# A mixture-of-experts kernel whose head and tail are laid out anew: token blocks loaded and summed during the first unit, two load queues, and two of the last groups read back a unit later

## The chip, the cores and the metric

The kernel runs on one core of a Trainium2 chip. The metric is the device time of one execution in microseconds (us). Engines are named as in the profile: PE is the matrix engine TensorE, PEld its weight loads, DVE is VectorE, ACT is ScalarE, POOL is GpSimd, SP is SyncE, which here issues most of the DMA transfers.

## The reference

A gated feed-forward layer with eight experts and one shared expert is added to its input. All is fp32; x is 16 sequences of 256 tokens with 256 features, and the hidden width F is 1024.

```python
g = jnp.einsum('bsd,edf->ebsf', h, Wg)
u = jnp.einsum('bsd,edf->ebsf', h, Wu)
expert_outs = jnp.einsum('ebsf,efd->ebsd', jax.nn.silu(g) * u, Wd)
expert_output = jnp.einsum('be,ebsd->bsd', gating_probs, expert_outs)
shared = jnp.einsum('bsf,fd->bsd', jax.nn.silu(h @ Sg) * (h @ Su), Sd)
sg = shared_gate_prob[:, :, None]
return x + (1.0 - sg) * expert_output + sg * shared      # h is x
```

Every expert runs over every token; the gates are given as one number for each expert and sequence.

## The kernel before

**Units.** The work is cut into 72 units: 9 experts (the shared one last) x 2 halves of the hidden width (512 columns, four chunks of 128) x 4 groups `g0` to `g3` of four token blocks (one block is one sequence of 256 tokens). The group runs fastest, so a set of weights serves four units in a row. A unit has an up part (`unit_up`, L590), which makes the gated hidden values, and a down part (`unit_down`, L677), which multiplies them by the down weights; the down part of one unit lies between the up matmuls of the next.

**Up.** A contraction of 256 is two halves of 128. Four weight chunks against four token blocks would take 32 products of 128x256 for each of the gate and up matrices. The kernel evaluates chunks and blocks at the points -1, 0, 1, 2 and takes 26: eight on the diagonal (`diagonal`, L515, into the PSUM bank D) and three for each of six pairs (`offdiagonal`, L558). Of a pair, one product goes to a bank M; POOL subtracts two diagonal terms (`s<-pq,pq`), DVE adds the two into a bank X (`X<-M,s`), and two more products accumulate on X. ACT takes the silu (`sg<-X`), DVE multiplies (`h<-X,coef,sg`). This needs sums of weights (`load_base` L285 and `make_pair` L306, tags wb and wp, made anew for each expert half) and of tokens (`make_xd` L387, tag xd, after a transpose on PE; `make_xp` L470, tag xp: for each of six pairs two 128x256 operations of DVE, one of POOL, for some pairs a scaling on ACT). The token sums are made once for each group, in the first units; `keep` (L376) writes them to DRAM, and `load_xd` and `load_xp` read them back in every later unit.

**Unit 0** alone is done plainly, so that TensorE can begin before any sums exist: eight steps (`unit_up`, `n == 0`), each with one product of a gate chunk (bank X) and one of an up chunk (bank M) with two token blocks, four 128x512 matmuls by the profile for each. `make_raw` (L424) transposes and copies its four blocks, `load_raw` (L328) brings the raw second halves of the first weights. Until data comes, 16 matmuls on zeros run (L258).

**Down.** In a 2x2 block scheme seven products are made instead of eight (`ORDER`, L674), each into one of two PSUM banks dn. ACT copies a product to SBUF (`ev<-dn`, L729), and two DMAs of POOL for each unit (`total<-ev`, L743) accumulate four and three of them in DRAM, in one total for each group. In the last expert half (units 68 to 71) the totals are read back (`load_pieces` L759), into the buffers wb and wd (`IN_W`) for g0, g2 and into ev (`IN_EV`) for g1 and g3. For units 68, 69 and 70 the unit's own seven products are added to these pieces by DVE straight from the dn banks. `finish` (L786) makes seven combinations of the pieces (128x512 each, two on POOL and five on DVE), transposes the results back on PE (`dn<-...` L829), adds x on DVE (L838) and stores. For the last unit, the combinations, transposes and x are done ahead (`basis`), and `last_down` (L851) adds plain down products, in the banks dn and M by turns, and stores.

**What sets the order.** Nothing is ordered by hand. Every instruction is an operation of a `Plan` (L47) with an engine, an estimated length, a lag, a rank, buffers and dependencies. `Plan.run` simulates the engines, takes on each the ready operation of lowest rank whose buffers are free, and emits in that order; PE strictly follows rank. A unit is W = 12 ranks long. The resulting order on each engine and queue is fixed in the program. Ranks for the loads, sums and transposes are given in the main loop (L879 to L916), e.g.

```python
    make_raw(a, -14 + 3 * a)                                    # unit 0
    (make_xd if n < NG else load_xd)(g, a, r0 - W + 6 * a - 4)  # all others
```

so before the change the blocks of g1 and g2 are transposed two at a time (`a` is a pair of blocks), mostly in the unit before the one that uses them, and the six xp of g1 are made around the start of unit 1, of g2 around unit 2, of g3 around unit 3; those of g0, which unit 0 does not need, are made at its end for the use in unit 4.

Of the kernel before, what the change touches and what calls it, by code (L numbers as in the profile page):

```python
# [16 lines left out]
P = 128  # L17
# [17 lines left out]
class Op:  # L35
    def __init__(self, engine, length, lag, rank, emit, deps, new, uses):
        self.engine, self.length, self.lag, self.rank, self.emit = engine, length, lag, rank, emit
        self.new, self.uses = new, uses
        self.after = []
        self.missing = 0  # L40
# [6 lines left out]
class Plan:  # L47
# [9 lines left out]
    HOP = 0.25  # L57

# [7 lines left out]
    def add(self, engine, length, rank, emit, deps=(), new=(), uses=(), lag=None):  # L66
        lag = self.HOP if lag is None else lag
        op = Op(engine, length, lag, rank, emit, deps, list(new), list(uses))
        for b in [*op.new, *op.uses]:
            b.users += 1  # L70
        self.ops.append(op)
        return op

    def run(self):
# [19 lines left out]
        now = 0.0  # L94
        while left:
# [9 lines left out]
            for e in ready:  # L105
# [23 lines left out]
                idle[e] = end  # L129
                order.append(took)  # L130
# [17 lines left out]
def kernel(  # L148
# [56 lines left out]
    tags("xp", [P, 3, TB], 5)  # L205
# [52 lines left out]
    for n in range(16):  # L258
# [4 lines left out]
    def load(rank, dst, src, kb, deps=(), new=(), uses=(), lag=None):  # L263
        return add("SP", 0.6, rank, lambda: nc.sync.dma_start(dst(), src), deps, new, uses, lag=lag or 3 + kb / 150)
# [20 lines left out]
    def load_base(m, e, half, rank):  # L285
# [5 lines left out]
        lag = None if rank < 0 else 14  # L291
        u = load(rank, lambda: b[:, :, 0, :], src[0], 256, [], [b], lag=lag)
        v = load(rank, lambda: b[:, :, 1, :], src[1], 256, [], [], [b], lag=lag)
# [12 lines left out]
    def make_pair(m, e, half, k, rank):  # L306
# [15 lines left out]
        if d == 1:  # L322
            o = tt("POOL", rank, lambda: b[:, 1:3, :], rr, uu, ALU.subtract, 2 * P, [r, u], [], [b, w])
        else:
# [3 lines left out]
    def load_raw(rank):  # L328
# [4 lines left out]
                rank + 3 * m, lambda m=m: b[:, :, m, :],  # L333
                sources(0)[m][ts(1, P), 0 : 4 * P].rearrange("p (c q) -> p c q", q=P), 256,
                [], [b] if m == 0 else [], [b] if m else [],
# [5 lines left out]
    def load_down(e, half, rank):  # L341
# [3 lines left out]
            n: load(rank, lambda n=n: b[:, :, n, :], s[:, :, c, k, :], 128, [], [b] if n == 0 else [], [] if n == 0 else [b], lag=12)  # L345
# [30 lines left out]
    def keep(key, b, deps, rank, kb):  # L376
        d = dram.tile(list(b.shape), F32, tag=f"keep_{key}", name=f"keep_{key}")
        kept[key] = d
        keptop[key] = add(
            "SP", 0.6, rank, lambda: nc.sync.dma_start(d, b.buf.tile), deps, uses=[b.buf], lag=2.2 + kb / 200  # L380
        )

    class Shaped:
        def __init__(self, buf, shape):
            self.buf, self.shape = buf, shape

    def make_xd(g, a, rank):  # L387
        b = Buf("xd", f"xd_{g}_{a}")
        done = {}
        for n in range(2):  # L390
            i = 2 * a + n
            t = POINTS[i]
            xin = Buf("xio", f"xin_{g}_{i}")
            src = x[4 * g + i].rearrange("(h p) d -> p h d", p=P)
            ld = load(rank - 1, lambda xin=xin: xin[:, :, :], src, 256, [], [xin])
            pt = Buf("dn", f"xt_{g}_{i}")

            def transposes(pt=pt, xin=xin):
# [4 lines left out]
            tr = add("PE", 4 * TR, rank, transposes, [ld], [pt], [xin])  # L403
            y = add(
                "ACT", act(TB), rank, lambda n=n, pt=pt: nc.scalar.copy(b[:, 2 + n, :], pt[:, 1, :]), [tr],
                [b] if n == 0 else [], [pt] if n == 0 else [pt, b],
            )
            if t == 0:
                o = add(
                    "ACT", act(TB), rank, lambda n=n, pt=pt: nc.scalar.copy(b[:, n, :], pt[:, 0, :]), [tr, y],  # L410
                    [], [pt, b],
                )
            else:
                o = stt(
                    rank, lambda n=n: b[:, n, :], lambda n=n: b[:, 2 + n, :], -float(t),
# [4 lines left out]
        keep(f"d_{g}_{a}", Shaped(b, [P, 4, TB]), [o for v in done.values() for o in v], rank + 2, 512)  # L420
# [3 lines left out]
    def make_raw(a, rank):  # L424
# [3 lines left out]
        for n in range(2):  # L428
# [3 lines left out]
            ld = load(rank - 1, lambda xin=xin: xin[:, :, :], src, 256, [], [xin])  # L432
# [9 lines left out]
            def copy(n=n, pt=pt):  # L442
                (nc.vector.tensor_copy if n else nc.scalar.copy)(b[:, n : n + 3 : 2, :], pt[:, :, :])
# [3 lines left out]
                    ("ACT", "DVE")[n], act(2 * TB), rank, copy, [tr],  # L447
# [5 lines left out]
    def sum_raw(a, rank, after):  # L453
# [14 lines left out]
        keep(f"d_0_{a}", Shaped(b, [P, 4, TB]), [o for v in done.values() for o in v], rank + 1, 512)  # L468
# [495 lines left out]
```

## Time and profile before

The kernel took 2561.29 us (median of 3 runs, 2561.25 to 2561.4).

| profiled execution | us |
|---|---|
| its own time | 2560.55 |
| its span, first to last instruction | 2558.8 |
| PE busy | 2521.2 (99%) |
| DVE busy | 1894.3 (74%) |
| POOL busy | 1721.5 (67%) |
| ACT busy | 778.3 (30%) |
| a unit in the middle (start to start) | 34.46 |
| unit 0 / 1 / 2 / 3 | 53.72 / 46.60 / 41.43 / 37.37 |
| unit 69 / 70 / 71 with the drain | 40.46 / 40.35 / 58.25 |
| mean granted TensorE clock | 0.997 |

A profile row such as `X<-M,s 128x512` names the written tile, then those read, by their tags (a buffer's number is left out). `xN` is the number of instructions. Times are in us, the mean of a group in ns. "Idle before, releaser" is how long the engine had stood still and what ended it. In the table, a unit begins with its first matmul on the sums of pairs (`M<-xp,wp`), so the unit that comes first holds everything from the start of the span; matmuls are pipelined, and the pitch from start to start is what one takes of the engine's time.

### The profile page before, as it was taken

What the parts mean: (1) busy time and instruction counts of PE and PEld (TensorE: products, weight loads), DVE (VectorE), ACT (ScalarE), POOL (GpSimd) and SP (SyncE); (2) the same over time, 40 slices, a digit from 0 to 9 for tenths busy, and PEclk for the clock granted to TensorE, in tenths of its full rate; (3) what the DMA queues carried; (4) which work ended last, traced back from release to release, by engine and by line L of the source; (5) the groups of instructions that cost most, each with busy time, mean ns of one, the idle gap of its engine ahead of it and who ended that gap; (6) DMA issues with size and microseconds to landing.
All of it is one profiled execution on the core that took longest, in us unless ns stands there. A gap on an engine that the chain in (4) does not pass through costs nothing. (4 is left out here: it accounts for less than half of the span.)

```text
span 2558.8 us, 30286 instructions
## 1 busy us (share of the span) xinstructions
PE 2521.2 (99%) x9644; PEld 1822.6 (71%) x9644; DVE 1894.3 (74%) x3272; ACT 778.3 (30%) x1367; POOL 1721.5 (67%) x1638
## 2 busy tenths in 40 slices
PE   8899999999999999999999999999999999999998
PEld 4667777777777777777777777777777777777766
DVE  5886777777676877676777767677867776776787
ACT  2333333333233333323333332333333233333310
POOL 5686766767676767676766767576767676776653
PEclk9999999999999999999999999999999999999999
DMA  6455666666666666666666666656666666666652
GB/s 200 163 181 166 166 157 169 161 175 159 174 157 158 162 161 175 158 175 156 166 162 168 168 167 163 166 151 164 165 168 168 162 168 158 166 160 177 181 184 85
DMA packets 179089, 421.51 MB, mean 165 GB/s; under 512 B 15056, under 2 KB 84192, under 8 KB 170224
## 3 DMA queue, kind: packets, MB, share of 16 engines
q1 hardware_dynamic: 159280, 294.70, 34.9%
q0 software_dynamic: 19648, 124.86, 26.5%
q8 instruction: 76, 1.25, 0.2%
q14 instruction: 85, 0.70, 0.1%
HBM read 276.90 MB, written 142.61 MB: 164 GB/s over the span
## 5 line engine op out<-in xcount | busy, mean ns | idle before, releaser
L268 POOL TENSOR_TENSOR s<-pq,pq 128x512 f32<-128x512 f32 x852 | 1147.9, 1376 | 523.1 <-DVE X L268 502.9
L509 PE MATMUL dn<-h,wd 128*128 128x512 f32 x1988 | 1016.6, 593 | 0.0
L509 PE MATMUL X<-xp,wp 128*128 128x256 f32 x3408 | 878.2, 380 | 7.4 <-DVE X L268 7.4
L268 DVE TENSOR_TENSOR X<-M,s 128x512 f32<-128x512 f32 x852 | 590.6, 694 | 367.5 <-PE M L509 236.8
L509 PEld LDWEIGHTS X<-xp,wp 128*128 128x128 f32 x3408 | 647.8, 190 | 219.5 <-issue 108.1
L509 PE MATMUL D<-xd,wb 128*128 128x256 f32 x2272 | 584.6, 380 | 4.5 <-DVE h L273 3.4
L509 PEld LDWEIGHTS M<-xp,wp 128*128 128x128 f32 x1704 | 324.2, 190 | 345.7 <-issue 332.3
L273 DVE SCALAR_TENSOR_TENSOR h<-X,coef,sg 128x256 f32<-128x256 f32 x852 | 394.8, 478 | 214.3 <-PE X L509 163.8
L509 PE MATMUL M<-xp,wp 128*128 128x256 f32 x1704 | 507.7, 380 | 0.0
L729 ACT COPY ev<-dn 128x512 f32<-128x512 f32 x476 | 279.4, 587 | 666.8 <-PE dn L509 666.6
L509 PEld LDWEIGHTS D<-xd,wb 128*128 128x128 f32 x2272 | 431.6, 190 | 67.6 <-DVE h L273 4.3
L268 DVE TENSOR_TENSOR h<-h,h 128x512 f32<-128x512 f32 x426 | 468.6, 1126 | 0.0
L509 PEld LDWEIGHTS dn<-h,wd 128*128 128x128 f32 x1988 | 377.8, 190 | 51.5 <-POOL wb L268 0.2
L607 ACT ACTIVATE sg<-X 128x512 f32<-128x512 f32 x434 | 258.4, 595 | 149.9 <-PE X L509 124.9
L536 ACT COPY pq<-D 128x512 f32<-128x512 f32 x284 | 166.5, 586 | 440.8 <-PE D L509 432.2
L268 DVE TENSOR_TENSOR pq<-D,pq 128x256 f32<-128x256 f32 x568 | 224.0, 417 | 40.4 <-PE D L509 40.1
L743 POOL DMA_DIRECT2D total<-ev x128 | 113.1, 883 | 195.7 <-ACT ev L729 186.8
L268 POOL TENSOR_TENSOR h<-h,h 128x512 f32<-128x512 f32 x142 | 199.7, 1407 | 47.8 <-PE dn L509 31.0
L607 ACT ACTIVATE sg<-D 128x512 f32<-128x512 f32 x142 | 84.8, 597 | 472.9 <-DVE pq L268 472.9
L268 POOL TENSOR_TENSOR wp<-wb 128x128 f32<-128x128 f32 x216 | 140.4, 661 | 0.0
L273 DVE SCALAR_TENSOR_TENSOR h<-D,coef,sg 128x256 f32<-128x256 f32 x284 | 134.5, 474 | 0.0
L273 DVE SCALAR_TENSOR_TENSOR wp<-wb,wp 128x256 f32<-128x256 f32 x108 | 88.3, 819 | 0.0
(68 smaller groups left out, 501.7 us busy)
## 6 DMA issues: line engine op xcount, KB each, us to landing
xp<-keep_p SPq DMA_DIRECT2D x408, 384.0 KB, 4.0
total<-ev POOLq DMA_DIRECT2D x68, 1024.0 KB, 7.9
xd<-keep_d SPq DMA_DIRECT2D x136, 512.0 KB, 3.5
total<-ev POOLq DMA_DIRECT2D x68, 768.0 KB, 7.0
keep_p<-xp SPq DMA_DIRECT2D x24, 384.0 KB, 2.6
wb<-in_L_cond_Wg_dram SPq DMA_DIRECT2D x33, 256.0 KB, 4.5
wb<-in_L_cond_Wu_dram SPq DMA_DIRECT2D x33, 256.0 KB, 4.9
wd<-in_L_cond_Wd_dram SPq DMA_DIRECT2D x64, 128.0 KB, 3.7
```

Of the source, the lines that this page charges most:

```text
L268: return add(engine, length, rank, lambda: eng.tensor_tensor(o(), a(), b(), op), deps, new, uses)
L273: lambda: nc.vector.scalar_tensor_tensor(o(), a(), c() if callable(c) else c, b(), ALU.mult, op),
L509: lambda: nc.tensor.matmul(o(), w(), mv(), start=start, stop=stop, skip_group_check=onto),
L536: lambda: nc.scalar.copy(p_[:, 2 - 2 * a : 4 - 2 * a, :], bank[:, :, :]), ps,
L607: lambda: nc.scalar.activation(b[:, :, :], bank[:, :, :], AF.Silu), deps, [b], [bank],
L729: lambda ev=ev, at=at, bank=bank: nc.scalar.copy(ev[:, at, :], bank.tile.rearrange("p a t -> p (a t)")),
L743: nc.gpsimd.dma_start(total[g][part], ev[:, 0:k, :], accum_op=ALU.add)
```

## The change

Parts, in the order of time:

1. **Start of the program.** 9 instead of 16 matmuls on zeros. The first loads get a new order over two queues: SP brings x0, x1, the raw Wg, the first half of Wu, x2, x3, the second halves of Wg and Wu, then the eight blocks of g1 and g2 (into h buffers), the down weights and the blocks of g3; the queue of ACT brings the first half of Wg and the raw Wu. All four copies of raw tokens are on ACT (two were on DVE).
2. **Order on PE in unit 0.** x0 and x1 are transposed, then step 0 follows, then x2 and x3, then the other steps at a spacing of 2.6 ranks (it was 2). Between them the eight blocks of g1 and g2 are transposed one at a time (before, six blocks of unit 0 in pairs of two). From g3 on, a block has its own rank too (`rank + n / 2`).
3. **Token sums.** The six xp of g1 are made in unit 0 into xp buffers, those of g2 into ev buffers ("aside") and stored at once, to be read back for unit 2. g0's are made ahead of unit 4. Six xp buffers instead of five. For the first weights only, three pairs of each matrix are made with an ACT multiplication and a POOL subtraction in place of one DVE operation.
4. **End.** Units 68 and 69 (g0, g1) use the normal `unit_down` (copies on ACT, accumulating DMAs of POOL); the totals are read back a unit later, into wb and wd (`IN_W`). Unit 70 (g2) still adds to pieces, in ev. g3's pieces go to wb and wd. A third one of the seven combinations goes to POOL (`o` = 2), the output transposes have a rank and spacing of their own, and `last_down` uses the banks X and M.
5. **The planner.** Transfers carry their size (`kb`), and the simulation sends them one after the other; lags of loads change with it. This adds no instruction.

The numbers of matmuls and transposes are unchanged but for the zeros. Cut to its core (left out: the planner's bookkeeping, the lags of `load_down`, `keep` and stores, lines that only follow a renamed argument, and the class `Slice`, a 128x3x256 view of a part of an ev buffer):

```diff
@@ tags
-    tags("xp", [P, 3, TB], 5)
+    tags("xp", [P, 3, TB], 6)
...
@@ zero matmuls
-    for n in range(16):
+    for n in range(9):
...
@@ load
-    def load(rank, dst, src, kb, deps=(), new=(), uses=(), lag=None):
-        return add("SP", 0.6, rank, lambda: nc.sync.dma_start(dst(), src), deps, new, uses, lag=lag or 3 + kb / 150)
+    def load(rank, dst, src, kb, deps=(), new=(), uses=(), late=0, engine="SP"):
+        queue = {"SP": nc.sync, "ACT": nc.scalar}[engine]
+        return add(
+            engine, 0.5, rank, lambda: queue.dma_start(dst(), src), deps, new, uses, lag=2.2 + late, kb=kb
+        )
...
@@ load_base
-    def load_base(m, e, half, rank):
+    def load_base(m, e, half, rank, ranks=None):
...
-        lag = None if rank < 0 else 14
-        u = load(rank, lambda: b[:, :, 0, :], src[0], 256, [], [b], lag=lag)
-        v = load(rank, lambda: b[:, :, 1, :], src[1], 256, [], [], [b], lag=lag)
+        late = 0 if rank < 0 else 8
+        ru, rv = ranks or (rank, rank)
+        engine = "ACT" if ranks and m == 0 else "SP"
+        u = load(ru, lambda: b[:, :, 0, :], src[0], 256, [], [b], late=late, engine=engine)
+        v = load(rv, lambda: b[:, :, 1, :], src[1], 256, [], [], [b], late=late)
...
@@ make_pair
+        elif e == half == 0:
+            o = add(
+                "ACT", act(2 * P), rank, lambda: nc.scalar.mul(b[:, 1:3, :], uu(), float(d)), [r, u], uses=[b, w]
+            )
+            o = tt("POOL", rank, lambda: b[:, 1:3, :], rr, lambda: b[:, 1:3, :], ALU.subtract, 2 * P, [o], [], [b])
...
@@ load_raw
-    def load_raw(rank):
+    def load_raw(ranks):
...
-                rank + 3 * m, lambda m=m: b[:, :, m, :],
+                ranks[m], lambda m=m: b[:, :, m, :],
...
-                [], [b] if m == 0 else [], [b] if m else [],
+                [], [b] if m == 0 else [], [b] if m else [], engine=("SP", "ACT")[m],
...
@@ make_xd
-    def make_xd(g, a, rank):
+    def make_xd(g, a, rank, load_rank, sum_rank):
...
-            xin = Buf("xio", f"xin_{g}_{i}")
+            xin = Buf("h" if g < 3 else "xio", f"xin_{g}_{i}")
...
-            ld = load(rank - 1, lambda xin=xin: xin[:, :, :], src, 256, [], [xin])
+            ld = load(load_rank, lambda xin=xin: xin[:, :, :], src, 256, [], [xin])
...
-            tr = add("PE", 4 * TR, rank, transposes, [ld], [pt], [xin])
+            rank_n = rank + n / 2
+            tr = add("PE", 4 * TR, rank_n, transposes, [ld], [pt], [xin])
...
-                    rank, lambda n=n: b[:, n, :], lambda n=n: b[:, 2 + n, :], -float(t),
+                    sum_rank, lambda n=n: b[:, n, :], lambda n=n: b[:, 2 + n, :], -float(t),
...
@@ make_raw
-    def make_raw(a, rank):
+    def make_raw(a, rank, load_rank):
...
-            ld = load(rank - 1, lambda xin=xin: xin[:, :, :], src, 256, [], [xin])
+            ld = load(load_rank, lambda xin=xin: xin[:, :, :], src, 256, [], [xin])
...
-                (nc.vector.tensor_copy if n else nc.scalar.copy)(b[:, n : n + 3 : 2, :], pt[:, :, :])
+                nc.scalar.copy(b[:, n : n + 3 : 2, :], pt[:, :, :])
...
-                    ("ACT", "DVE")[n], act(2 * TB), rank, copy, [tr],
+                    "ACT", act(2 * TB), rank, copy, [tr],
...
@@ make_xp
-    def make_xp(g, k, rank):
+    def make_xp(g, k, rank, put_aside=False):
...
-        b = Buf("xp", f"xp_{g}_{k}")
+        if put_aside:
+            new = k % 2 == 0
+            buf = aside[g, k // 2] = Buf("ev", f"aside_{g}_{k}") if new else aside[g, k // 2]
+            b = Slice(buf, k % 2)
+        else:
+            new = True
+            buf = b = Buf("xp", f"xp_{g}_{k}")
...
-            [s, yj], uses=[b, tj],
+            [s, yj], uses=[buf, tj], more=0.3,
...
-        xp[g, k], xpop[g, k] = b, (s, n7, n6)
-        keep(f"p_{g}_{k}", Shaped(b, [P, 3, TB]), [s, n7, n6], rank + 2, 384)
+        if not put_aside:
+            xp[g, k], xpop[g, k] = b, (s, n7, n6)
+        keep(f"p_{g}_{k}", [P, 3, TB], b, buf, [s, n7, n6], rank + 2, 384)
...
@@ unit_up, n == 0
-                    r = 2 * step - 7 + m / 2
+                    r = 2.6 * step - 7 + m / 2
...
@@ finish
-    def finish(g, pieces, rank, store_it=True):
+    def finish(g, pieces, rank, out_rank, store_it=True):
...
-                "POOL" if o in (3, 4) else "DVE", rank, m[o][0], m[a][0], m[c][0], op, 2 * TB,
+                "POOL" if o in (2, 3, 4) else "DVE", rank, m[o][0], m[a][0], m[c][0], op, 2 * TB,
...
-                r = rank + 2 + (2 * row + bp) / 2
+                r = out_rank + 0.6 * (2 * row + bp)
...
@@ last_down
-            bank = Buf(("dn", "M")[step % 2], f"ld_{blk}_{h}")
+            bank = Buf(("X", "M")[step % 2], f"ld_{blk}_{h}")
...
@@ main loop
     for n, unit in enumerate(units):
         e, half, g = unit
         r0 = W * n
+        if n == 0:
+            make_raw(0, -14, -20)
+            load_base(0, e, half, -16, (-20, -16))
+            first_raw = load_raw((-19, -17.5))
+            load_base(1, e, half, -15, (-18, -15))
+            make_raw(1, -5.5, -17)
+        elif g == 0:
+            for m in range(2):
+                load_base(m, e, half, r0 - W + 3 * m - 8)
         if g == 0:
-            for m in range(2):
-                load_base(m, e, half, r0 - W + 3 * m - (8 if n else 4))
-                if n == 0 and m == 0:
-                    first_raw = load_raw(-12.5)
             for k in range(len(PAIRS)):
                 for m in range(2):
                     make_pair(m, e, half, k, r0 + 2 * k + m - (8 if n else -4))
             load_down(e, half, r0 + W - 8)
         if n == end:
             rows = load_rows(e, half, r0 - 2)
-        for a in range(2):
-            if n == 0:
-                make_raw(a, -14 + 3 * a)
-            else:
-                (make_xd if n < NG else load_xd)(g, a, r0 - W + 6 * a - 4)
+        if n == 1:
+            for a in range(2):
+                make_xd(g, a, -3.4 + 2 * a, -14, -3 + 2 * a)
+            for k in range(len(PAIRS)):
+                make_xp(g, k, 5 + k)
+            for a in range(2):
+                make_xd(2, a, 3.2 + 2 * a, -13, 5 + 2 * a)
+            for k in range(len(PAIRS)):
+                make_xp(2, k, 11 + k / 2, True)
+        elif n == 3:
+            for a in range(2):
+                make_xd(g, a, r0 - W + 6 * a - 4, r0 - W + 6 * a - 6, r0 - W + 6 * a - 7)
+            for k in range(len(PAIRS)):
+                make_xp(g, k, r0 + 2 * k - 5)
+        elif n == 4:
+            for a in range(2):
+                load_xd(g, a, r0 - W + 6 * a - 4)
+            for k in range(len(PAIRS)):
+                make_xp(g, k, r0 + 2 * k - 5)
+        elif n:
+            if n > 2:
+                for a in range(2):
+                    load_xd(g, a, r0 - W + 6 * a - 4)
+            for k in range(len(PAIRS)):
+                load_xp(g, k, r0 + 2 * k - 5)
         if n == end:
-            basis = finish(g, load_pieces(g, IN_EV, r0 - 2 * W + 3), r0 - 2 * W + 7, False)
-        if n:
-            for k in range(len(PAIRS)):
-                (make_xp if n < NG else load_xp)(g, k, r0 + 2 * k - 5)
+            basis = finish(g, load_pieces(g, IN_W, r0 - 2 * W + 1), r0 - 2 * W + 4, r0 - 2 * W + 10.3, False)
         hb, hops = unit_up(n, unit)
-        if n == 0:
-            for k in range(len(PAIRS)):
-                make_xp(g, k, 10 + k)
         if n == end:
             last_down(n, unit, hb, hops, rows, basis)
+        elif n == end - 1:
+            pieces = load_pieces(g, IN_EV, r0 + W - 1)
+            unit_down(n, unit, hb, hops, pieces)
+            finish(g, pieces, r0 + 2 * W + 1, r0 + 2 * W + 4.2)
         elif n > end - NG:
-            pieces = load_pieces(g, IN_EV if g == 1 else IN_W, r0 + W - 3)
-            unit_down(n, unit, hb, hops, pieces)
-            finish(g, pieces, r0 + 2 * W + 1)
+            unit_down(n, unit, hb, hops)
+            finish(g, load_pieces(g, IN_W, r0 + 2 * W + 2), r0 + 2 * W + (4, 11)[g], r0 + 2 * W + (11, 13.5)[g])
         else:
             unit_down(n, unit, hb, hops)
     last = {}
```

## The prediction

> **What bounds the kernel now.** I read the busy shares first, then the starts of the units, then the waits of TensorE in the few units that are longer than the rest. TensorE is busy all but 1% of the span:
>
> ```profile
> PE 2521.2 (99%) x9644; PEld 1822.6 (71%) x9644; DVE 1894.3 (74%) x3272; ACT 778.3 (30%) x1367; POOL 1721.5 (67%) x1638
> ```
>
> So no gain is to be had from the 65 units in the middle. A unit's start is its first M matmul in TensorE's timeline; cutting the span there gives this table of windows (length; busy of TensorE, its weight loads, DVE, ACT, POOL; clock; DMA share; GB/s). Rows 1 to 4 are units 1 to 4, row 5 is unit 68, the last three are units 69, 70 and 71 with the drain:
>
> ```profile
> 53.72:100.32 46.60, 38.20 (x146) 26.39 (x145) 41.10 (x74) 13.82 (x28) 30.79 (x31) 0.96 0.52 193
> 100.32:141.75 41.43, 37.24 (x141) 26.77 (x140) 33.01 (x57) 12.68 (x24) 23.80 (x22) 0.96 0.51 178
> 141.75:179.12 37.37, 34.92 (x133) 24.91 (x132) 34.46 (x54) 11.41 (x21) 32.13 (x37) 1.00 0.51 178
> 179.12:213.59 34.47, 34.47 (x134) 25.08 (x133) 25.10 (x45) 10.90 (x19) 21.94 (x20) 1.00 0.44 154
> 2385.28:2419.74 34.46, 34.46 (x133) 25.08 (x132) 23.18 (x43) 10.90 (x19) 19.41 (x16) 1.00 0.64 160
> 2419.74:2460.20 40.46, 37.88 (x149) 27.42 (x148) 35.66 (x59) 6.91 (x12) 21.39 (x17) 0.96 0.62 188
> 2460.20:2500.55 40.35, 36.81 (x150) 26.39 (x148) 34.88 (x58) 6.90 (x12) 22.70 (x16) 1.00 0.63 203
> 2500.55:2558.80 58.25, 48.91 (x201) 35.16 (x199) 43.20 (x66) 4.18 (x7) 21.79 (x16) 0.97 0.24 78
> ```
>
> A full unit takes 34.46. Useful work of the others, from TensorE's pitch (start to start: 1.72 for four 128x512, 0.86 for four 128x256, 0.434 for the four transposes of a token block): unit 0, 16 plain products x 1.72 + 8 D x 0.86 + 10 blocks x 0.434 = 38.7; units 1 and 2, 34.46 + 2 blocks = 35.3; units 69 and 70 36.2; unit 71 45.7 and a drain of 3.45 from its last matmul to the end. What is above that is lost: 15.0, 11.3, 6.1, 2.9 in units 0 to 3 and 4.2, 4.2, 9.1 in units 69 to 71. These 52.8 us are all that the change can reach; the floor is the start (below), near 2518.
>
> In unit 0, TensorE's timeline (start, length, idle before and its releaser) shows 13.2 us lost ahead of the first plain product (14.98 less four transposed blocks, 1.74):
>
> ```profile
> 13.25 1.94 PE L438 MATMUL dn<-ident,xio 128*128 128x128 f32 x8 [3.49 <-DMA xio<-in_x_dram]
> 14.98 2.49 PE L509 MATMUL X<-pq,wb 128*128 128x512 f32 x4
> ```
>
> In units 1 and 2 the waits name DVE. The last of 4.19 us, at 110.71, begins with one DVE operation of two SBUF inputs, stretched from 0.42 to 4.18 while POOL ran four operations back to back:
>
> ```profile
> 101.63 4.18 DVE L273 SCALAR_TENSOR_TENSOR xp<-xd,xp 128x256 f32<-128x256 f32 x1
> ...
> 102.36 0.73 POOL L268 TENSOR_TENSOR xp<-xd,xp 128x256 f32<-128x256 f32 x1
> 103.04 1.27 POOL L268 TENSOR_TENSOR s<-pq,pq 128x512 f32<-128x512 f32 x1
> 104.27 1.26 POOL L268 TENSOR_TENSOR h<-h,h 128x512 f32<-128x512 f32 x1
> ```
>
> At the end, TensorE's waits (total, times, longest) are all for DVE too:
>
> ```profile
> PE X L509 <- DVE X L268: 4.0, 3, 2.6
> PE dn L829 <- DVE xd L268: 3.1, 3, 1.6
> PE dn L829 <- DVE wb L268: 3.0, 2, 2.8
> PE dn L829 <- DVE ev L268: 1.9, 1, 1.9
> ```
>
> **The change, part by part.** *Start.* Seven of 16 zero matmuls go; they end at 5.95 and the first block comes at 7.15, so nothing follows. The first four blocks and four weight blocks, eight transfers of 256 KB, are ordered so that step 0 needs six and the last two are x2 and x3. Before, the DMA share is 0.76 in the first 10 us and 1.03 in the next 10: a second queue adds no rate, only the order and two earlier issues. The eighth block of that size landed at 13.11. So TensorE streams from about 13.5, with four blocks (1.74) and step 0 (3.44) behind it: 8.3 lost instead of 13.2. If the two queues put x3 behind two more blocks (14.75) it is 9.9; below 8.3 only if the transfers start faster than before.
>
> *Unit 0.* Twelve blocks are transposed instead of ten (39.6 of work). DVE loses the two raw copies to ACT (2 x 0.68) and six weight sums; it gains the sums of two groups: 33 operations of two SBUF inputs instead of 27. POOL gains six 128x256 sums (0.776) and 6 token sums (about 0.85): from some 28 to 36 us, and it can't begin before Wg's second half has landed (13.9 before, where it now is ninth or tenth). What such a pair of engines costs each other is the open term. By the page: "SBUF — State Buffer", section Who interferes with whom, has the second SBUF input of DVE and a POOL operation that reads SBUF exclude each other for one whole instruction. The rows here show worse:
>
> ```profile
> L273 DVE SCALAR_TENSOR_TENSOR xp<-xd,xp 128x256 f32<-128x256 f32 x18 | 20.0, 1109 | 0.7 <-ACT xp L482 0.4
> L268 DVE TENSOR_TENSOR xp<-xd,xd 128x256 f32<-128x256 f32 x12 | 10.4, 868 | 0.0
> ```
>
> Alone these take about 0.41, so the means hide some that wait for three or four POOL operations (4.18). Bounds for the mean: 0.42 (never in the way) and 1.11 (the upper row). The rule, one POOL operation of 0.7 to 1.3 met half way and by some of them, gives 0.75; I take that, because a sum that runs beside a waiting POOL costs the 0.42. Units 0 and 1 hold 44 such operations after the change (33 + 11) and DVE work without them of 12.5 + 16.9: 29.4 + 44 x 0.75 = 62.4, against TensorE's 68.9 from 13.5 on (39.6 - 5.2 + 34.5). It fits at 91%, not smoothly. I put unit 0's stalls at 5.0: 1.7 as before, 2.5 for order, 0.8 for the clock. On the clock the trace and a page differ: "TensorE: Matmul & The Clock Gate", Part 1, has the slow clock return after an idle window of about 3.4 us; here it was granted at 0.5 in five windows of 3.41 us, at 12.78, 57.15, 111.77, 2446.5 and 2511.3, each after a window in which TensorE was busy up to 41%, at a cost near 1.7 each. By the rule the new start (idle about 2 us before step 0, and again before x3) has none; by the rows it may have one; I take half. Unit 1 then starts at 39.6 + 8.3 + 5.0 = 52.9 instead of 53.7: gain 0.8, with two more blocks done.
>
> *Units 1 to 4.* Unit 1 has no transposes and no sums of g2: 34.46 + 2.0 (the longest wait of this kind left, 1 to 3) instead of 46.60: 10.1. Unit 2 still transposes two blocks of g3: 35.3 + 0.5 instead of 41.43: 5.6. It reads g2's six sums back (384 KB each, 4.0 us to landing in the table of issues) while unit 4 no longer reads g0's six: SP's number is unchanged. Unit 3 keeps g3's sums on DVE (19 two-input operations instead of 17, POOL 30 us as before): 38.0, a loss of 0.6. Unit 4 makes g0's sums (17 operations): DVE has 9 us spare in row 4, so between 0 and 3 lost, as in unit 3; I take 1.0. Start and units 0 to 4: 0.8 + 10.1 + 5.6 - 0.6 - 1.0 = 14.9.
>
> *End.* For g0 and g1, 14 additions from PSUM leave DVE (0.68 each, 9.6 in all, the bank held until the piece is read back) and become 14 ACT copies (0.587) and four POOL accumulating DMAs (0.883). ACT is busy 6.9 of 40 there, so the banks come free sooner. The pieces are read back a unit later: the accumulation lands in 7.0 to 7.9 (at most 10.7), the read takes 3 to 6, and the plan leaves some 14 us more than both. They stand on SP behind token loads and before the sixth xp of the last unit, which would be late next. One combination per group (1.0 to 1.3 on DVE) goes to POOL, 1.3 to 1.5, where it is on the way to the first transposes. DVE in unit 69 falls from 22.6 + 12 two-input operations to 17.8 + 10, in unit 70 from 23.2 + 11 to 18.4 + 10; unit 71 has 26.6 + 14 against 25.4 + 15. With one output block moved into unit 71: units 69 and 70, 35.8 + 0.7 = 36.5 each, 4.0 and 3.9 less. Unit 71: 46.6 + 3.45 + 3.7 = 53.7, 4.5 less; the 3.7 are the transposes of g1 and g2, which still wait for combinations and for two dn banks (9.1 before; 0 to 7). The final products' move to X and M banks frees dn and costs nothing: X is idle by then. Sum 12.4.
>
> **Total**: 14.9 + 12.4 = 27.3. The profiled execution took 2560.55 for a span of 2558.8; so span 2531.5, execution 2533.3, and with the median 0.74 above the profiled one, 2534.0.
>
> **Rivals.** *A: DVE and POOL bound the start.* If the two-input operations take the upper row's 1.11, DVE needs 29.4 + 44 x 1.11 = 78.2 in units 0 and 1, 9.3 over TensorE's 68.9, and with 6 of order it loses 15 where I set 7: gain 19, 2542. For it: DVE was busy 41.1 of 46.6 in unit 1. Against: unit 1 then held 30 such operations and keeps 11, and the six sums of each group in unit 0 have some 35 us to spread over. *B: the stalls nearly all go*: units 0 to 4 lose 2, the end 3 us less than I allow: gain 35 to 40, 2521 to 2526; the middle units show that with 6 to 12 such operations TensorE waits for nothing. *C: the end gives little*, because a read back is late or the combinations on POOL (67% busy) hold the transposes: tail 3 instead of 12.4, 2543. *D, slower:* POOL starves DVE in unit 0. Its place is the sums of g1 and g2 between the plain steps, with POOL's 36 us queued since 14. It decides where 29.4 + 44 m exceeds 68.9 + 7 + 27.3, at m = 1.67; at 2.0, 2575. Single cases reached 4.18, no group of this shape has a mean over 1.11. That two queues change nothing is in the bounds of the start (1.6).
>
> **How the numbers follow.** My case 0.60 (2527 to 2541: start 0 to 1.6, units 0 to 4 by 4 either way, the end by 4), A 0.20, B 0.12, C 0.05, D 0.03. The range 2522 to 2547 takes in A, C and most of B. About 0.2% (5 us) is what a measurement here can tell from no change. Faster: all but D and A's far end, 0.96; within 0.2%: 0.01; slower: 0.03.
>
> **What would show it.** First plain product near 10 to 11.5 and x3's transposes near 13.5; starts of units 1 to 5 near 53, 89.5, 125, 163, 198.5; the mean of two-input sums near 0.75; units 69 to 71 near 36.5, 36.5, 53.7; no wait of TensorE on a dn addition of DVE in units 69 and 70. Wrong if the first M comes after 58, if unit 3 or 4 grows by more than 4, or if the output transposes wait for reads from memory.

## The result

The changed kernel takes 2534.72 us (median of 4 runs, 2534.18 to 2535.56), the kernel before 2561.27; the ratio is 0.9897, 95% interval 0.988 to 0.9914. The forecast was 2534.0. The medians differ by 26.6. The profiled execution, the slowest of the four, took 2535.56 with a span of 2533.8, which is 25.0 less than before; the tables below are of this one.

Busy shares of the changed kernel, from its page:

```profile
PE 2513.3 (99%) x9637; PEld 1817.8 (72%) x9637; DVE 1866.6 (74%) x3246; ACT 789.0 (31%) x1389; POOL 1722.7 (68%) x1652
```

Its windows by unit, cut as before (units 1 to 5, unit 68, then 69, 70 and 71 with the drain):

```profile
52.33:87.63 35.30, 34.75 (x138) 24.94 (x137) 29.37 (x50) 11.15 (x21) 23.76 (x24) 1.00 0.50 168
87.63:123.89 36.26, 35.56 (x142) 25.78 (x141) 27.50 (x53) 12.07 (x23) 22.22 (x20) 1.00 0.57 192
123.89:160.65 36.76, 35.27 (x134) 24.83 (x133) 36.16 (x56) 11.63 (x21) 33.09 (x36) 1.00 0.35 132
160.65:198.80 38.15, 35.26 (x133) 24.83 (x132) 34.67 (x54) 11.52 (x21) 27.00 (x26) 1.00 0.52 184
198.80:233.27 34.47, 34.47 (x134) 25.08 (x133) 23.57 (x43) 10.90 (x19) 22.73 (x20) 1.00 0.58 169
2370.48:2404.94 34.46, 34.46 (x133) 25.08 (x132) 23.18 (x43) 10.90 (x19) 19.43 (x16) 1.00 0.60 151
2404.94:2442.00 37.06, 36.05 (x146) 26.17 (x145) 29.65 (x49) 11.03 (x20) 24.02 (x20) 1.00 0.73 202
2442.00:2477.78 35.78, 35.78 (x147) 26.25 (x146) 27.32 (x49) 10.79 (x20) 24.60 (x20) 1.00 0.72 194
2477.78:2533.80 56.02, 48.29 (x210) 35.10 (x208) 42.06 (x65) 3.94 (x7) 23.50 (x19) 1.00 0.58 189
```

Against the forecast:

| unit | before | forecast | after | gain forecast | gain measured |
|---|---|---|---|---|---|
| 0 | 53.72 | 52.9 | 52.33 | 0.8 | 1.4 |
| 1 | 46.60 | 36.5 | 35.30 | 10.1 | 11.3 |
| 2 | 41.43 | 35.8 | 36.26 | 5.6 | 5.2 |
| 3 | 37.37 | 38.0 | 36.76 | -0.6 | 0.6 |
| 4 | 34.47 | 35.5 | 38.15 | -1.0 | -3.7 |
| 69 | 40.46 | 36.5 | 37.06 | 4.0 | 3.4 |
| 70 | 40.35 | 36.5 | 35.78 | 3.9 | 4.6 |
| 71, drain | 58.25 | 53.7 | 56.02 | 4.5 | 2.2 |
| sum | | | | 27.3 | 25.0 |

Start of the program, TensorE's timeline of the changed kernel:

```profile
1.20 3.96 PE L265 MATMUL X<-zero 128*128 128x512 bf16 x9 [1.20 <-DVE zero L238]
4.99 0.60 PE L461 MATMUL dn<-ident,xio 128*128 128x128 f32 x4
7.23 0.66 PE L461 MATMUL dn<-ident,xio 128*128 128x128 f32 x4 [1.64 <-DMA xio<-in_x_dram]
8.56 3.57 PE L541 MATMUL X<-pq,wb 128*128 128x512 f32 x4 [0.67 <-ACT pq L466]
11.96 1.88 PE L541 MATMUL M<-pq,wb 128*128 128x512 f32 x4
13.68 1.04 PE L461 MATMUL dn<-ident,xio 128*128 128x128 f32 x8
14.56 1.88 PE L541 MATMUL X<-pq,wb 128*128 128x512 f32 x4
```

The first plain product starts at 8.56 instead of 14.98 but takes 3.57 where the later ones take 1.88: the clock was granted at 0.5 from 8.38 to 11.79. Here is that stretch with the one of the same length before it (the last three figures of a line are the clock, the DMA share and GB/s):

```profile
4.97:8.38 3.41, 1.28 (x9) 0.80 (x8) 0.00 (x0) 1.04 (x2) 0.00 (x0) 1.00 1.10 219
8.38:11.79 3.41, 3.23 (x4) 1.51 (x5) 0.56 (x2) 0.13 (x1) 0.00 (x0) 0.50 0.99 288
```

That is the only such stretch left of five (the last 1.6 us of the drain apart). At half the clock 3.41 us cost at most 1.7, so by my estimate the four that are gone make up to 6.8 of the 25.0 us; the forecast had them inside the losses of their units. The transposes of x2 and x3 at 13.68 wait for nothing: x3 landed at 12.40.

TensorE's longest waits in the first 160 us of the kernel before, in the first 205 us of the changed kernel, and in its last three units:

```profile
PE dn L401 <- DVE xd L273: 8.1, 3, 4.2
```

```profile
PE X L541 <- DVE X L277: 4.3, 4, 1.4
PE D L541 <- ACT sg L639: 1.9, 2, 1.0
PE dn L461 <- DMA xio<-in_x_dram: 1.6, 1, 1.6
```

```profile
PE dn L862 <- DVE xd L277: 2.9, 3, 1.9
PE X L541 <- DVE X L277: 1.8, 3, 1.0
```

The 8.1 us for transposes that waited for `xd` are gone. Three of the four waits on `X` lie in unit 4.

### The profile page after: what moved, and what is told of

Same layout as the page of the kernel before. It is cut to its first block, busy times and chain, and to the rows that moved or that the text cites. A ratio compares the mean times of both kernels' runs of the same rounds, so it can differ in the third digit from the quotient of the medians.

```text
span 2533.8 us, 30307 instructions
## 1 busy us (share of the span) xinstructions
PE 2513.3 (99%) x9637; PEld 1817.8 (72%) x9637; DVE 1866.6 (74%) x3246; ACT 789.0 (31%) x1389; POOL 1722.7 (68%) x1652
## 5 line engine op out<-in xcount | busy, mean ns | idle before, releaser
L761 ACT COPY ev<-dn 128x512 f32<-128x512 f32 x490 | 287.8, 587 | 681.1 <-PE dn L541 681.1
L277 DVE TENSOR_TENSOR h<-h,h 128x512 f32<-128x512 f32 x426 | 453.5, 1090 | 0.0
```

The source lines that it names most:

```text
L277: return add(engine, length, rank, lambda: eng.tensor_tensor(o(), a(), b(), op), deps, new, uses)
L761: lambda ev=ev, at=at, bank=bank: nc.scalar.copy(ev[:, at, :], bank.tile.rearrange("p a t -> p (a t)")),
```

## Experiments

**The two halves alone.** The first is the changed kernel with the end of the kernel before, the second the kernel before with the new end (in both, the parts of `finish`, `last_down` and the main loop for units 68 to 71 are exchanged whole):

```diff
@@ head_only (against the changed kernel)
-        elif n == end - 1:
-            pieces = load_pieces(g, IN_EV, r0 + W - 1)
...
+            pieces = load_pieces(g, IN_EV if g == 1 else IN_W, r0 + W - 3)
+            unit_down(n, unit, hb, hops, pieces)
+            finish(g, pieces, r0 + 2 * W + 1, r0 + 2 * W + 3)
@@ tail_only (against the kernel before): the same lines the other way round
```

> The changed kernel with the end of the kernel before (units 68 to 70 add their products to pieces on DVE, five combinations of seven on DVE, the old ranks, last products in dn and M). By the two traces the head gains 14.9 us up to the start of unit 5 (233.27 instead of 248.05) and the end 10.2. If the two halves are independent: 2546.4 +- 1, the first five units as in the changed kernel (starts 52.3, 87.6, 123.9, 160.7, 198.8) and units 69 to 71 as before (40.5, 40.4, 58.3). Rival: the shift of the head alters the order at the end too, then units 69 to 71 differ from the kernel before by more than 1 us in sum.

Measured: 2545.45 (2544.18 to 2546.99; ratio 0.9939, 0.9925 to 0.9954). Unit 5 starts at 197.97 instead of 213.59; from there to the end it takes 2345.2, as the kernel before. (The two figures 233.27 and 248.05 of the expectation are the starts of unit 6; those of unit 5 are 198.80 and 213.59, with the same difference.) The head is worth 15.6 here and does not touch the end: units 69 to 71 take 139.1 in sum, as before.

> The kernel before with the end of the changed kernel alone. Independent halves: 2561.3 - 10.2 = 2551 +- 1, units 69 to 71 at 37.1, 35.8 and 56.0, the head as before (unit 1 at 53.7, unit 5 at 248.0). Rival: the gain at the end needs the changed kernel's planner, then it is smaller by more than 2 us.

Measured: 2547.60 (2545.96 to 2549.02; ratio 0.9947, 0.9932 to 0.9962), a miss. From the start of unit 5 to the end it takes 2330.4, 14.8 less than before, where the same end in the changed kernel gains 10.2. (Its head is 2.9 longer than that of the kernel before, unit 5 starting at 216.53: in this execution the clock was at 0.5 for 17.1 us ahead of unit 5, there for 10.2. So only the part from unit 5 on is compared.) Unit 69 takes 35.78 instead of 37.06 and the last 52.65 instead of 56.02. So the new end was worth more than I forecast (12.4), and the changed kernel lost 4.6 of it again. `late_g1` below looks for that.

**The start.** 16 zero matmuls instead of 9, and one queue instead of two:

```diff
-    for n in range(9):
+    for n in range(16):
@@ one_queue
-        queue = {"SP": nc.sync, "ACT": nc.scalar}[engine]
+        engine, queue = "SP", nc.sync
```

> The changed kernel with 16 instead of 9 zero matmuls. Theory of the clock: with nine, TensorE idles 1.6 us between the transposes of x0 and x1 and 0.7 before the first plain product, and the clock was granted at 0.5 from 8.38 to 11.79; seven more fill that gap (they end near 6.5 to 7.1, x1 lands at 7.2), no such stretch follows, unit 1 starts 1.7 us earlier (50.6) and the time is 2533.0, or 0.5 to 1.7 less than the changed kernel's. Rival: the zeros only delay the transposes of x0 and the clock falls anyway: 2534.7 to 2535.5.

Measured: 2534.54 (2534.24 to 2534.89; ratio 0.9897). The profiled run shows no slow stretch, and the mean clock was 1.000 in all four. But in three of the changed kernel's four runs it was 1.000 too: the slow stretch comes in some executions only. The zeros end at 7.2, delay the first product to 8.93, and unit 1 starts at 51.65 instead of 52.33:

```profile
8.93 1.98 PE L541 MATMUL X<-pq,wb 128*128 128x512 f32 x4 [0.73 <-ACT pq L466]
```

Three other runs have the head of the changed kernel with nine zeros and, in their profiled executions, no slow stretch in it: `late_g1`, `head_only` and `comb2_dve` start unit 1 at 51.28 to 51.52. So the slow stretch delayed unit 1 by 0.8 to 1.05 in its execution, and the seven zeros more give 0.1 to 0.4 of that back. The clock theory holds for the single execution (0.7 us of the expected 1.7) and gives the median nothing.

> The changed kernel with all loads on SP's queue, in the same order of ranks. If the rate of the transfers is the limit and only their order counts, the eighth block of 256 KB lands within 0.4 us of 12.40 and the time stays within 0.5 us of 2534.7. Rival: the second queue brings the first transfers 0.5 us sooner each because SP issues one in 0.5 us; then the first plain product starts near 9.2 to 9.6 instead of 8.56 and the time is 0.6 to 1.0 longer.

Measured: 2534.55 (2533.14 to 2536.53; ratio 0.9899). The eighth block landed at 12.23, and the median didn't change. On one queue the transfers land one after the other (x0 at 3.62, x1 at 4.34, the first half of Wg at 8.00); on two they share the rate (4.74, 7.18, 5.35). The first product starts at 8.13:

```profile
8.13 1.96 PE L541 MATMUL X<-pq,wb 128*128 128x512 f32 x4 [1.85 <-DMA wb<-in_L_cond_Wg_dram]
```

Two runs with a mean clock under 1.000 took 2535.6 and 2536.5, the other two 2533.1 and 2533.5. The changed kernel's three runs at 1.000 took 2534.2 to 2535.0, so at the full clock one queue is the faster by about 1.2, and unit 1 starts at 49.87 against the 51.28 to 51.52 above. The second queue brings nothing and seems to cost about a microsecond. Since one queue starts the first product as early as two, what moved it from 14.98 is the order of the loads and of TensorE's own work; no run parts these two.

**Where g0's sums are made.** Back to the end of unit 0; and, in unit 4, the POOL part of these sums given to DVE:

```diff
@@ g0_old
-        elif n == 4:
-            ...
-                make_xp(g, k, r0 + 2 * k - 5)
...
+        if n == 0:
+            for k in range(len(PAIRS)):
+                make_xp(g, k, 10 + k)
@@ n6_dve
-            "POOL", rank, lambda: b[:, 2, :], ...
+            "DVE" if g == 0 else "POOL", rank, lambda: b[:, 2, :], ...
```

> The changed kernel with g0's own pair sums made at the end of unit 0 and stored, as before, and read back for unit 4. If unit 4 is longer (38.15 against 34.46) because of these sums on DVE and POOL, it falls to 34.5, and units 0 and 1 take over the cost: 12 more DVE operations of two SBUF inputs at about 0.75 in a unit with 6 us of DVE to spare, 3 to 4 us longer: 2534 to 2536 in all. Rival: DVE and POOL starve each other when 44 such operations become 56 there; units 0 and 1 grow by more than 7, the time is 2538 or more.

Measured: 2549.81 (2549.47 to 2550.55; ratio 0.9955, 0.9938 to 0.9971), far above the first theory. Unit 4 does fall to 34.46, but unit 1 takes 54.83. The rival has the sign and not the cause. TensorE's waits of that kernel in the first 140 us, and the timelines of DVE and ACT in unit 1:

```profile
PE D L541 <- ACT pq L568: 14.7, 2, 14.5
```

```profile
71.45 0.42 DVE L277 TENSOR_TENSOR xp<-pq,pq 128x256 f32<-128x256 f32 x1 [0.86 <-DMA keep_p<-xp]
...
75.80 0.43 DVE L277 TENSOR_TENSOR xp<-pq,pq 128x256 f32<-128x256 f32 x1 [3.02 <-DMA keep_p<-xp]
76.70 0.43 DVE L282 SCALAR_TENSOR_TENSOR xp<-pq,xp 128x256 f32<-128x256 f32 x1 [0.48 <-ACT xp L513]
```

```profile
77.74 0.58 ACT L568 COPY pq<-D 128x512 f32<-128x512 f32 x1 [1.07 <-POOL xp L277]
```

The sums shown take 0.42 or 0.43 each (the longest of these in the unit 1.31, at 60.46), so POOL does not starve DVE here. They wait for xp buffers, which come free only as stores end, since g1's six sums now lie in that ring too. g0's tokens stay in pq buffers meanwhile, and the copy `pq<-D` for unit 2 starts only when POOL's sum that reads them is done (77.7); until then the one D bank is full and TensorE stands for 14.5 us. The two waits on stores are 3.9 of it; the rest is the other work of DVE, POOL and ACT that stands between these sums. After the stall the clock was at 0.5 until 82.92, in which 4.5 us of matmuls ran at half speed, another 2.3 lost. With g1's sums made in unit 0, g0's can't stay where they were: their move to unit 4 is worth 15 us, the 3.7 that unit 4 loses already taken off.

> The changed kernel with the POOL part of g0's six pair sums (128x256, about 0.88 on POOL) on DVE instead: for unit 4 six more DVE operations of two SBUF inputs and six fewer POOL operations. It measures what DVE and POOL cost each other there: in unit 4 of the changed kernel 17 such DVE operations take 1.13 us in the mean, alone 0.41 to 0.68. If POOL's six operations are what stretches them, the mean falls below 0.9 and unit 4 stays at or under 38.15 although DVE has six operations more (2534.0 to 2534.7). If they are not (the steady s<-pq,pq and h<-h,h of POOL do it), DVE gets 2.5 to 6 us more and unit 4 goes to 40 or more (2537).

Measured: 2535.30 (2533.80 to 2535.52; ratio 0.9897). Unit 4 takes 39.23, but the profiled execution had a slow stretch of the clock in it (175.50 to 178.91, 1.7 us lost); the one run at a mean clock of 1.000 took 2533.80. The groups of DVE in unit 4, of the changed kernel and of this one:

```profile
L277 DVE TENSOR_TENSOR h<-h,h 128x512 f32<-128x512 f32 x7 | 9.6, 1396 | 0.0
L282 DVE SCALAR_TENSOR_TENSOR xp<-xd,xp 128x256 f32<-128x256 f32 x3 | 3.2, 1067 | 0.0
```

```profile
L277 DVE TENSOR_TENSOR h<-h,h 128x512 f32<-128x512 f32 x7 | 7.4, 1084 | 0.0
L277 DVE TENSOR_TENSOR xp<-xd,xp 128x256 f32<-128x256 f32 x4 | 1.8, 452 | 0.0
```

The mean of the two-input operations of the unit falls from 1.13 to 0.74, their sum from 19.2 to 16.3, with five more of them (22 instead of 17). That mean is lowered by the added operations too; without the four of them that lie in the unit (1.8) it is 14.5 for 18, or 0.81. The same seven `h<-h,h` fall from 9.6 to 7.4 and would take 4.8 at the 0.68 of one alone. So POOL's six operations make roughly half of the stretch, and POOL's other work the rest: both theories are true in part. As for the unit's length, the run leaves it open whether the trade is worth making.

**Three smaller parts undone.** Transposes in pairs; the first weights' sums on DVE; the combination `o` = 2 on DVE:

```diff
@@ pairs_t
-            rank_n = rank + n / 2
+            rank_n = rank
@@ stt_back
-        elif e == half == 0:
+        elif False:
@@ comb2_dve
-                "POOL" if o in (2, 3, 4) else "DVE", ...
+                "POOL" if o in (3, 4) else "DVE", ...
```

> The changed kernel with the transposes of g1, g2 and g3 two blocks at a time instead of singly. In the kernel before, TensorE waited 8.1 us for transposes of pairs in units 1 and 2, with dn banks shared with the down products. If the pairs are the cause, units 1 and 2 lose 2 to 4 us (2537 to 2539). If the cause was only DVE's stretched operation (4.18) that held the bank, with g1's and g2's sums gone from these units the pairs cost under 1 us: 2534.5 to 2535.5.

Measured: 2537.59 (2536.54 to 2538.23; ratio 0.9908, 0.9891 to 0.9924). Units 1 and 2 take 37.19 and 37.96, 3.6 more together, and a wait is back:

```profile
PE dn L423 <- DVE xd L282: 3.3, 2, 2.4
```

Both waits are for blocks of g3, which still lie in these units. Pairs are the cause, as the first theory has it; it fits that two blocks take both dn banks, among the down products that need them. In unit 0 the pairs cost nothing (unit 1 starts at 50.26, in the three runs named above at 51.28 to 51.52), so the whole is only 2.9 longer.

> The changed kernel with the six 128x256 weight sums of the first expert on DVE again, in place of six ACT multiplications and six POOL subtractions. If DVE is what units 0 and 1 wait for, six more operations of 0.4 to 0.9 there cost 1 to 3 us (2535.7 to 2537.7). If POOL is (36 us of work in unit 0, holding DVE off), six POOL operations of 0.82 less gain about 1 (2533.7).

Measured: 2533.99 (2533.92 to 2534.04; ratio 0.9892). Neither theory stands out: against the changed kernel's runs at the full clock (2534.2 to 2535.0) it is about 0.5 less, and units 0 and 1 end at 86.41 (86.93 with 16 zeros and a full clock). DVE's two-input operations in unit 0 are six more at a mean of 0.74 instead of 0.72. DVE had the room; moving these sums to ACT and POOL gained nothing.

> The changed kernel with the combination o = 2 of each of the last groups on DVE (0.68 alone) instead of POOL (1.27). By the chain that ends last, DVE's own order sets the end and this combination on POOL is early: then four more on DVE cost 0.7 to 1.4 us in the last unit (2535.4 to 2536.1). Rival: POOL's combinations stretch those of DVE (1.44 instead of 0.68, twice in the last unit) by more than they take off it; then the time is 0.5 to 1 less (2534).

Measured: 2534.75 (2534.65 to 2534.93; ratio 0.9896). Unit 70 takes 0.4 more, the last 0.4 less. But the last unit takes the same 55.59 in `n6_dve` and `stt_back`, which leave this combination on POOL, so that 0.4 is no effect of the edit. Neither theory is borne out: where this combination stands makes no difference that these runs can tell.

**What the end lost, and versions beyond the change.** `late_g1` alters one number of the planner. `best1` adds to it the single load queue and 12 zero matmuls, `best2` also makes g0's sums in units 1 and 2:

```diff
@@ late_g1 (load_pieces)
-                ..., late=3,
+                ..., late=-2 if g == 1 else 3,
@@ best2 (n == 1)
+            for a in range(2):
+                load_xd(0, a, 18 - 2.5 + a)
+            for k in range(len(PAIRS)):
+                make_xp(0, k, 18 + 2 * k)
@@ best2 (n == 4: the branch goes, xd and xp are read back as in every unit)
```

> The changed kernel with one number of the planner changed: the extra lag of the loads that read g1's pieces back is -2 instead of 3, so the plan has them land about 5 us sooner, and DVE's combinations of g1 stand earlier in its order. No instruction is added or removed. Theory: the last unit is 3.4 us longer than in the kernel with the old head (56.0 against 52.65) only because these combinations are late in DVE's order (first at 27.4 us after the unit's start, though the pieces landed at 20.0; 21.1 in the other); then the unit with its drain comes to 52.6 to 53.5 and the time to 2531.3 to 2532.3. Rival: they aren't late by order but wait for POOL's combinations or dn banks; then the unit stays at 55.5 to 56.5 and the time at 2534.5.

Measured: 2532.89 (2532.48 to 2532.99; ratio 0.9888). DVE's first two combinations of g1 in the changed kernel, and in this one (whose last unit starts at 2476.70):

```profile
2505.14 0.68 DVE L277 TENSOR_TENSOR wb<-wb,wd 128x512 f32<-128x512 f32 x1
2506.13 0.68 DVE L277 TENSOR_TENSOR wd<-wd,wb 128x512 f32<-128x512 f32 x1
```

```profile
2496.21 0.68 DVE L277 TENSOR_TENSOR wb<-wb,wd 128x512 f32<-128x512 f32 x1
2498.25 0.68 DVE L277 TENSOR_TENSOR wd<-wd,wb 128x512 f32<-128x512 f32 x1
```

They start 19.5 us after the unit's start instead of 27.4, and the last unit with its drain takes 53.99 instead of 56.02. So 2.0 of the 3.4 us were an order fixed by the plan: its simulation let the last piece land 27.6 us after the unit's start, where the trace of the changed kernel has 20.0. The other 1.4, and the 1.3 of unit 69 (a late `X`), stay open.

> Three changes to the changed kernel together: all loads on SP's queue (unit 0 ended 1.8 us sooner in that run), 12 zero matmuls (so that TensorE doesn't fall to the slow clock before the first product), and the lag of g1's read back at -2. Additive: 2534.7 - 1.8 - 1.8 + 0.4 = 2531.5. If the single queue's gain was the clock alone, 2532.9 as with the lag alone.

Measured: 2531.84 (2531.75 to 2532.11; ratio 0.9885, 0.9871 to 0.99): 1.0 less than with the lag alone. It matches the additive 2531.5 more nearly than the 2532.9. All four runs had the full clock, and so had the four of `late_g1`, so this 1.0 is not the clock: it is the single queue or the three zeros more, and zeros alone gained nothing in `zeros16`.

> The same three, and g0's pair sums made in units 1 and 2 (from a reload of its xd, one every two ranks from rank 18) and stored, to be read back for unit 4. Units 1 and 2 have 6 and 9 us of DVE to spare, unit 4 of the changed kernel lost 3.7. If the sums fit there, unit 4 comes to 34.5, units 1 and 2 grow by 0.5 to 1.5 together: 2.2 to 3.2 less than the kernel of this call without it, near 2529. Rival: xp buffers held by the temporary sums or stores delay the reads of unit 2 (a store held up DVE for 3.0 us where g0's sums were made in unit 1), and units 1 and 2 grow by 4 or more: 2532 or above.

Measured: 2529.15 (2528.31 to 2530.10; ratio 0.9875, 0.986 to 0.9889). Units 1 to 4 take 37.07, 36.79, 36.36 and 34.46 where `best1` has 35.65, 36.26, 36.75 and 38.16: 2.1 less in sum, the first theory. It is the fastest version here, 5.6 us below the changed kernel.

## Why the prediction was right

- *The start* (8.3 lost): measured 9.4 (13.68 less two blocks, 0.87, and step 0, 3.44), inside its bounds of 8.3 to 9.9, but not for the reason given, so that it fits is partly luck. "TensorE streams from about 13.5" when the eighth block lands is wrong: that block was in time (12.40). The first product came at 8.56, ahead of the 10 to 11.5 that I named as a sign, but step 0 took 5.12 where I had 3.44, because of the slow clock at 8.38; for that I had set half a stretch, 0.8, in the next term. In `late_g1`, without the slow stretch, x2 and x3 are transposed from 12.15: 7.8 lost, under my lower bound. On the clock the rows were the better guide than the rule that the prediction cites: TensorE had been busy for 1.28 of the 3.41 us before, with two groups of transposes, not idle. I also misread the zeros of the kernel before: they end at 7.15 (1.19 + 5.96), not at 5.95. x0 landed there at the same 7.15, so nothing followed from it; here x0 came at 4.74, and `zeros16` transposes it only at 7.16.
- *Unit 0's stalls* (5.0): 52.33 - 13.68 less 35.3 of work, so 3.4; my 5.0 had 0.8 for the clock in it. No starvation; the two-input operations of units 0 and 1 took (20.1 + 13.1) / 41 = 0.81 in the mean, where I took 0.75 and counted 44. Rivals A (1.11) and D (1.67) fall by this number.
- *Units 1 and 2* (10.1 and 5.6): 11.3 and 5.2. I had counted two transposed blocks in unit 1 before and none after. The traces have four before, so 10.4 were lost there and not 11.3, and two of g3 after (at 75.95 and 78.11), 0.87 of work that my 34.46 left out. The 2.0 that I allowed for a wait was mis-sized the other way (the one left is 0.55), so the 10.1 came near by two errors of opposite sign. `pairs_t` shows that 3.6 of the gain is due to single transposes, `g0_old` that the place of g0's sums is a condition for the rest. I had costed that move at 1.0 and given it no gain; without it the head loses what it gained.
- *Unit 4* (loss 1.0, at most 3): 3.7, the mis-sized term, just under the 4 that I had named as a sign of being wrong. I argued from DVE's 9 us to spare at 0.41 to 0.75 for an operation; the 17 took 1.13, the size of rival A. The stretch is seen in one line of DVE (0.68 when alone), with what POOL did meanwhile:

```profile
161.94 3.26 DVE L277 TENSOR_TENSOR h<-h,h 128x512 f32<-128x512 f32 x1
```

```profile
161.46 1.28 POOL L277 TENSOR_TENSOR s<-pq,pq 128x512 f32<-128x512 f32 x1
162.69 0.73 POOL L277 TENSOR_TENSOR xp<-xd,xp 128x256 f32<-128x256 f32 x1
163.37 1.27 POOL L277 TENSOR_TENSOR s<-pq,pq 128x512 f32<-128x512 f32 x1
```

- *Units 69 and 70* (7.9): 8.0. *The last unit* (4.5): 2.2, because its combinations are late in DVE's order: the 3.7 that I had for the transposes of g1 and g2 came to 6.0 (56.02 less 46.6 and 3.45), and `late_g1` takes 2.0 of it back. I had expected a read back that lands too late (rival C); it landed in time, and the plan believed otherwise. The end alone, in the old order, gives 14.8.
- The two misses in size, 2.7 and 2.3, are partly made up by units 0, 1, 3 and 70. The sum was closer than its terms. That the median came within 0.7 of the forecast is luck besides: the span missed by 2.3 (2533.8 for 2531.5), but the profiled execution lay 0.74 below its median before and 0.84 above it now.

## What to carry to other kernels

Where a list scheduler fixes each engine's order, a lag that is too long costs like one that is too short: compare the planned landing with the trace's, transfer by transfer. When work is moved forward into a full unit, look first for who holds the buffers until then (here pq and xp, 15 us), and only then at engine time. Where transposes share their banks with products that need them, try them one block at a time (here 3.6 us in two units; in unit 0 it gained nothing).

## What the runs showed of the hardware

A DVE operation of two SBUF inputs was stretched over three POOL operations in a row (3.26 us above) and over four (4.18 before), not over one; the Trainium skill, "SBUF — State Buffer", section Who interferes with whom, has the shared ports held for one whole instruction. Two load queues did not move the eighth block (12.40 against 12.23 with one), only when the blocks before it landed. The slow clock came in some executions of one program and not in others (with `n6_dve`, 2535.3 to 2535.5 at a mean clock of 0.999 and 2533.8 at 1.000), so two single profiles should not be compared for less than that.
